# A graph layer on one core: 640 instead of 512 edges of a part taken from resident tables

## The chip, the cores and the metric

One core of one Trainium2 chip. The metric is the device time of one execution in microseconds, median of several runs.

## The reference, cut to what matters

`x` has 12500 rows (nodes) of 128 numbers; there are 412500 edges, `src` to `dst`, sorted by `dst`. For each edge a small gate is computed from the difference of its two rows, and the gated differences are summed by target:

```python
theta = x[dst] - x[src]
w = sigmoid(relu(theta @ W1 + b1) @ W2 + b2)
agg = segment_sum(w * theta, dst)
indeg = segment_sum(1, dst)
out = layernorm(x + agg + indeg * (x @ W4 + b4))
```

Since W1 is linear, a table z in DRAM holds for each node its product with W1 beside its row; an edge then needs the z row of its source, and W1's product for its target.

## The kernel before, in words

**Parts and blocks.** The edges are cut into 276 consecutive *parts*; two parts make a *block*, whose targets lie in a window of 104 nodes. The first 18 parts are *plain*: 1024 edges each, all fetched by GpSimd with eight indirect gathers (L401, 128 rows each) into one of five `zbuf`. The 258 parts behind them hold CE = 1532 edges: 512 *hot* edges that are not gathered, and up to 1024 others in 128 x 8 slots that are (two slots of a pair share a target). Parts are fetched three or four ahead.

**Hot edges.** The first 8192 rows of x stand in SBUF as 32 tables of 256 rows, each split into three bf16 terms (`tabs`). A part takes 16 hot edges from each table, 8 from each of its two half lists. For eight parts and four tables at a time (a *fetch*, about one a part), the rows' numbers are loaded and spread over all partitions (`hot_load`), compared with the partitions' numbers (`hot_tiles`, L1039, tile `of`), and multiplied with the tables (`hot_products`, L1055: 24 bf16 matmuls into a PSUM bank `pd`). `hot_out` (L1069, ScalarE) copies the columns into `xT`, the 512 hot source rows of a part, turned. Per part then: `hot_turned` multiplies them with -W1 (L1105) and adds the targets' products by a one-hot (L1106) into the bank `pz`; `hot_relu` (L1111, ScalarE) makes `hr`; `hot_rows` multiplies `hr` with w2, four matmuls that give one column each (L1119), and turns the rows back (L1122); `hot_weights` takes the sigmoid of four columns (L1128) and weighs the rows (L1131, ScalarE).

**The gathered edges.** `spread_y` multiplies one-hots of the targets with their W1 products (L893); `logits` on VectorE subtracts, applies relu and w2, and sums (L951, L956, L962) and makes one-hots of the target nodes (L926); `weigh_rest` weighs the gathered rows on ScalarE (L993, `wx`). `add_block` and `begin_block` add all weighed rows of a block into the bank `pa` by these one-hots (L1158).

**Placing.** Which edges are hot is found on VectorE, for 64 parts at a time (a *set*; before there are five sets behind the plain parts: four of 64 parts and one of two), on 128 half lists in 128 partitions. In `place` a loop over the 32 tables raises the candidates of the next table above all others by an exclusive-or of some bits (L583), takes the eight largest (MAX, L586) and strikes them out (MATCH_REPLACE, L589). The generator yields after each piece; the main loop spends a *credit* on such pieces at the end of each part (2.5 a part, with costs of 0.85 for "k", 0.5 for "x", 2.5 to 3.5 for larger ones).

**Order.** `early_part(s)` writes out the order of the plain parts, `part(s)` that of the others, engine by engine: each engine takes its instructions in exactly that order. In `part(s)` the hot work is for part t = s + 1. `issue` interleaves the sums (L1158) with the table products (L1055) on TensorE in four pieces.

## Time and profile before

| | us |
|---|---|
| median of three runs (2940.52 to 2944.18) | 2941.33 |
| the profiled execution | 2943.8 |
| its span, first to last instruction | 2942.0 |
| TensorE busy / weight loads busy | 2548.2 / 2012.3 |
| VectorE / ScalarE / GpSimd busy | 2380.3 / 2123.8 / 2164.5 |

A row of a group names line, engine, operation, tiles and shapes, then count, busy time in us, mean ns of one, and the engine's idle time just before it with what ended it. In a timeline a row has the start, the time to the end of the last of its instructions, and in brackets the idle time before. A TensorE instruction's shown length is that of its way through the array; the spacing of starts is what a stream of them costs.

### The profile page before, as it was taken

How to read it: one execution, taken by the hardware profiler on the slowest of the kernel's cores; microseconds unless marked ns; L12 is line 12 of the kernel's file. 1: busy time of each engine (PE TensorE's matmuls, PEld its weight loads, DVE VectorE, ACT ScalarE, POOL GpSimd, SP SyncE). 2: the span in 40 equal slices, each digit the busy share in tenths (PEclk: the TensorE clock that was granted, in tenths of full speed). 3: DMA queues.
4: the chain of work that ended last, by engine and by line, in shares of the span. 5: the costliest groups of instructions: out<-in, count | busy, mean ns of one | idle time of the engine just before them, and what ended most of it. 6: DMA issues, size and time to landing. Idle time of an engine off the chain costs nothing.

```text
span 2942.0 us, 59129 instructions
## 1 busy us (share of the span) xinstructions
PE 2548.2 (87%) x18606; PEld 2012.3 (68%) x18606; DVE 2380.3 (81%) x4436; ACT 2123.8 (72%) x6416; POOL 2164.5 (74%) x2213
## 2 busy tenths in 40 slices
PE   6877899988888998998898888898998888888886
PEld 5656677777676777776776666676776666677764
DVE  7899699888957988888558888888568888888654
ACT  6365778767777777677777777776777777677776
POOL 4566777777777777777777777777777777777774
PEclk8688999989999999999999999999999999999998
DMA  8455555555554555554554545454554555555542
GB/s 285 151 153 123 142 139 138 140 135 137 140 146 134 137 140 140 133 141 135 143 150 133 135 133 141 132 141 134 143 142 128 140 132 141 133 138 141 141 134 77
DMA packets 239329, 413.58 MB, mean 141 GB/s; under 512 B 63423, under 2 KB 147226, under 8 KB 237470
## 3 DMA queue, kind: packets, MB, share of 16 engines
q0 software_dynamic: 105280, 286.93, 35.3%
q1 hardware_dynamic: 131756, 116.40, 15.3%
q10 hardware_dynamic: 1970, 6.40, 0.7%
q8 instruction: 148, 2.42, 0.3%
q14 instruction: 175, 1.43, 0.2%
HBM read 388.57 MB, written 20.94 MB: 139 GB/s over the span
## 4 chain that ended last, share of the span: by engine, by line
PE 38%; ACT 19%; DVE 15%; DMA 11%; issue 7%; POOL 1%; DVEq 0%; SPq 0%; ACTq 0%; POOLq 0%
PE pa L1158 14%; DMA zbuf<-z,src_i 10%; DVE zbuf L951 5%; PE y L893 5%; PE pd L1055 5%; ACT wx L993 5%; PE px L1119 4%; ACT wxh L1131 4%; PE pz L1105 3%; PE pz L1106 3%; PE pz L1122 3%; ACT oh L872 2%; ACT oh L873 2%; ACT xT L1069 1%; ACT a L1213 1%
## 5 line engine op out<-in xcount | busy, mean ns | idle before, releaser
L401 POOL DMA_INDIRECT zbuf<-z,src_i x2060 | 2018.5, 980 | 637.0 <-issue 236.6
L993 ACT ACTIVATE wx<-zbuf,wx 128x128 f32<-128x128 f32 x2060 | 630.2, 388 | 0.0
L1158 PE MATMUL pa<-wx,ow 128*104 128x260 f32 (+1 forms) x2284 | 628.4, 393 | 0.0
L893 PEld LDWEIGHTS y<-y,oh 128*128 128x128 f32 (+1 forms) x2156 | 276.1, 197 | 420.5 <-DVE zbuf L951 378.2
L1055 PEld LDWEIGHTS <-tabs 128*128 128x128 bf16 x6360 | 452.8, 101 | 124.2 <-issue 8.2
L951 DVE TENSOR_TENSOR zbuf<-y,zbuf 128x1024 f32<-128x1024 f32 x258 | 315.1, 1221 | 272.2 <-DMA zbuf<-z,src_i 270.9
L1055 PE MATMUL pd<-of,tabs 128*128 128x128 bf16 (+3 forms) x6360 | 535.2, 223 | 0.0
L1111 ACT ACTIVATE hr<-pz 128x512 f32<-128x512 f32 x258 | 152.9, 593 | 522.9 <-PE pz L1106 522.8
L893 PE MATMUL y<-y,oh 128*128 128x128 f32 (+1 forms) x2156 | 314.7, 291 | 228.7 <-DVE zbuf L951 220.6
L1158 PEld LDWEIGHTS pa<-wx,ow 128*104 128x104 f32 x2284 | 342.8, 179 | 40.6 <-issue 0.4
L962 DVE TENSOR_REDUCE lg<-zbuf 128x8 f32<-128x1024 f32 x273 | 329.8, 1208 | 13.2
L956 DVE SCALAR_TENSOR_TENSOR zbuf<-zbuf,fix 128x1024 f32<-128x1024 f32 x273 | 331.6, 1215 | 9.3
L1158 PE MATMUL pa<-wxh,owh 128*104 128x130 f32 x2064 | 329.0, 296 | 0.0
L1131 ACT ACTIVATE wxh<-pz,wxh 128x128 f32<-128x128 f32 x1032 | 295.2, 369 | 42.1 <-PE pz L1122 35.9
L1105 PE MATMUL pz<-xT,wni 128*128 128x512 f32 x516 | 278.5, 621 | 1.6 <-ACT wxh L1131 1.6
L1158 PEld LDWEIGHTS pa<-wxh,owh 128*104 128x104 f32 x2064 | 274.3, 186 | 0.0
L1119 PEld LDWEIGHTS px<-w_c,hr 128*128 128x128 f32 x2064 | 263.5, 200 | 7.8 <-ACT hr L1111 7.8
L1119 PE MATMUL px<-w_c,hr 128*128 128x1 f32 x2064 | 262.1, 248 | 5.6 <-ACT hr L1111 5.6
L1106 PE MATMUL pz<-oh,y 128*128 128x512 f32 x516 | 264.5, 594 | 0.1
L872 ACT ACTIVATE oh<-to_all,away,mine 128x512 f32<-128x512 bf16 (+1 forms) x257 | 213.6, 831 | 3.1 <-DMA to_all<-off_d 3.1
L1106 PEld LDWEIGHTS pz<-oh,y 128*128 128x128 f32 x516 | 98.2, 191 | 124.3 <-issue 123.4
L1122 PE MATMUL pz<-wni,xT 128*128 128x128 f32 x1032 | 176.3, 297 | 0.0
(304 smaller groups left out, 3595.8 us busy)
## 6 DMA issues: line engine op xcount, KB each, us to landing
to_all<-off_d SPq DMA_DIRECT2D x258, 128.0 KB
zbuf<-z,src_i POOLq DMA_INDIRECT x2060
hot_src<-hot_s SPq DMA_DIRECT2D x228, 128.0 KB
y<-z SPq DMA_DIRECT2D x270, 28.0 KB
xw<-in_x_dram SPq DMA_DIRECT2D x138, 52.0 KB
out_dram<-o SPq DMA_DIRECT2D x138, 52.0 KB
wx<-in_x_dram ACTq DMA_DIRECT2D x12, 512.0 KB
z<-zbuf SPq DMA_DIRECT2D x6, 1024.0 KB
```

The lines of the kernel that those rows point to most:

```text
L401: ins = nc.gpsimd.indirect_dma_start(out=rows_of(s)[:, k, :], out_offset=None, in_=z if s >= NH else x, in_offset=IndirectOffsetOnAxis(ap= ...
L893: nc.tensor.matmul(y[:, j, :], d["oh"][:, (k0 + j) * P:(k0 + j + 1) * P], y_of(s), start=True, stop=True)
L951: nc.vector.tensor_sub(half, yy.to_broadcast([P, 2, n, D]), half)
L956: nc.vector.scalar_tensor_tensor(h[:, at, :], h[:, at, :], 0.0, w2.to_broadcast([P, n, D]), op0=OP.max, op1=OP.mult)
L962: nc.vector.tensor_reduce(lg[:, at, 0], h[:, at, :], AX.X, OP.add)
L993: weighed[0] = nc.scalar.activation(wx[:, k, :D], rows_of(s)[:, k, D:], AF.Copy, scale=wx[:, k, D:D + 1])
L1055: steps_of.append(lambda q=q, i=i, t=t, j=j: nc.tensor.matmul(to[:, q], tabs[:, g, i, q, t, :], of[:, t, q], start=j == 0, stop=j == HT * ...
L1105: nc.tensor.matmul(pz, wneg, xT, start=True, stop=False)
L1106: nc.tensor.matmul(pz, y_of(t), blocks[t // SUB]["oh"][:, BP:], start=False, stop=True)
L1119: nc.tensor.matmul(lgh()[:, t % SUB, q:q + 1], hr[:, at], w2_c, start=True, stop=True)
L1131: nc.scalar.activation(wx[:, q, :D], pz[:, q * P:(q + 1) * P], AF.Copy, scale=wx[:, q, D:D + 1])
L1158: return [lambda i=i, one=one, w=w: nc.tensor.matmul(to if len(w.shape) == 3 else to[:, 0, :], one, w, start=first and i == 0, stop=last a ...
```

## The change

One more of every four tables is asked twice: of each group of four tables the first gives 32 hot edges a part instead of 16. That makes 640 hot edges a part, 320 in each half list, so that parts hold CE = 1608 edges and there are 246 instead of 258 behind the plain ones, in four sets (three of 64, one of 54). With it goes:

- **PSUM.** 640 columns of f32 don't fit into a bank. The products with W1 of the two half lists go to two banks, `pz` and `halves[1]` (named px in the rows), 320 columns each, in four matmuls instead of two; the one-hots of each half list stand on 64 of the 128 partitions, with the y rows loaded to both halves of the partitions (four loads a block). The same for the y matmuls of the gathered edges.
- **Logits.** Five matmuls with w2 repeated 32 times as weights and 128 columns of `hr` moving, each into a strip of 32 partitions of `pz`, instead of four that give a column each. A sigmoid over 256 columns (`hot_gates`, ScalarE), two transposes back (`hot_gates_turned`, TensorE), and a copy of five columns precede the weighing of five, not four, times 128 rows.
- **Table products.** Still 24 matmuls a fetch, of which six now have 256 columns; the fourth table's go to the end of `halves[1]`, copied out at the end of the part (`last_out`).
- **Order.** Sums and table products are no longer interleaved: logits, turning, table products, gate transposes, sums. `hot_out` comes before `hot_relu`.
- **Placing.** Forty pairs of MAX and MATCH_REPLACE instead of 32 a set, over 805 instead of 767 columns. The exclusive-or is a TENSOR_TENSOR with a constant column in PSUM (`steps_c`), except in the first set, where it stays a TENSOR_SCALAR. Credits 2.8 a part instead of 2.5 (6.5 instead of 5.5 in the plain parts).
- **One-hots of target nodes** in plain parts from the fifth on are made by ScalarE (Abs, then Relu, ten instructions a part) instead of two TENSOR_TENSOR on VectorE.
- **Room.** Two instead of three `wx`, three instead of four `hot_src`, four instead of five `xw`, one `owh`; hot rows are loaded two parts ahead of their tiles instead of three.

TensorE in the order of the program, before: one part between the table products of the part ahead and those of its own (tiles: `xT` hot rows, `oh` one-hots, `y` target rows and result, `hr` relu's output, `w_c` w2, `wni` -W1 and the identity, `pa` the block's sums).

```order
L1055 MATMUL pd<-of,tabs 128x16x8
L1105 MATMUL pz<-xT,wni 128x512
L1106 MATMUL pz<-oh,y_150 128x512
L893 MATMUL y<-y_145,oh 128x128 x4
L1119 MATMUL px<-w_c,hr 128x1 x4
L1122 MATMUL pz<-wni,xT 128x128 x4
L1158 MATMUL pa<-a,sh 104x130
L1158 MATMUL pa<-wxh,owh 104x130 x2
L1055 LDWEIGHTS tabs
L1055 MATMUL pd<-of,tabs 128x16x8
```

The same place of the changed program, from the end of one part's table products (the weight loads are L1094 LDWEIGHTS) to the start of the next ones:

```order
L1094 MATMUL px<-of,tabs 128x128
L1177 MATMUL pz<-wni,hr 128x128
L1180 MATMUL pz<-wni,hr 128x32
L1217 MATMUL pa<-a,sh 104x130
L1217 MATMUL pa<-wxh,owh 104x130 x10
L1217 MATMUL pa<-wx_79,ow 104x260 x4
L1148 MATMUL pz<-xT,wni 128x320
L1148 MATMUL px<-xT,wni 128x320
L1151 MATMUL pz<-oh,y_142 128x320
L1151 MATMUL px<-oh,y_142 128x320
L917 MATMUL y<-y_145,oh 128x128 x4
L1165 MATMUL pz<-hr,w_c 32x128 x5
```

All sums now stand in one run behind the gate transposes (L1177, L1180), and the node products are four instructions into two banks.

ScalarE in an even part, before, from the relu to the weighing of the gathered rows (`wxh` weighed hot rows, `lg` the gathered edges' logits):

```order
L1111 ACTIVATE hr<-pz 128x512
L1069 ACTIVATE xT<-pd 128x12x32
L1069 ACTIVATE xT<-pd 128x4x32
L872 ACTIVATE oh<-to_all,away,mine 128x512
L873 ACTIVATE oh<-oh 128x512
L1128 ACTIVATE wxh<-px,b_c 128x4
L1131 ACTIVATE wxh<-pz,wxh 128x128 x4
L975 ACTIVATE wx_79<-lg,b_c 128x8
L979 ACTIVATE wx_79<-rel 128x4
L993 ACTIVATE wx_79<-zbuf_179,wx_79 128x128 x8
```

and in the changed program:

```order
L1109 ACTIVATE xT<-pd 128x10x32
L1157 ACTIVATE hr<-pz 128x320
L1157 ACTIVATE hr<-px 128x320
L892 ACTIVATE oh<-to_all,away,mine 128x640
L893 ACTIVATE oh<-oh 128x640
L1172 ACTIVATE hr<-pz,b_c 128x256
L1187 ACTIVATE wxh<-pz 128x5
L1190 ACTIVATE wxh<-pz,wxh 128x128 x2
L1190 ACTIVATE wxh<-px,wxh 128x128 x3
L1109 ACTIVATE xT<-px 128x4x8
L1109 ACTIVATE xT<-px 128x12x8
L1009 ACTIVATE wx_78<-lg,b_c 128x8
```

The copies from `pd` moved ahead of the relu; the sigmoid of the gates (L1172) and the copies from px at the end are new.

The diff, cut to its core:

```diff
-CE = 1532
+CE = 1608
+RU = RG + 1
-HK = HR * HS
+HK = HR // RG * RU * HS
...
         for r in range(HR):
             if r:
-                v.tensor_scalar(bits, bits, ((r - 1) ^ r) << FIELD, None, op0=OP.bitwise_xor)
+                if i:
+                    k = ((r - 1) ^ r).bit_length() - 1
+                    v.tensor_tensor(bits, bits, steps_c[:, k:k + 1].to_broadcast([P, WL]), op=OP.bitwise_xor)
+                else:
+                    v.tensor_scalar(bits, bits, ((r - 1) ^ r) << FIELD, None, op0=OP.bitwise_xor)
                 yield "x"
-            eight = tops[:, r, :]
-            v.max(eight, left)
-            v.tensor_scalar(eight, eight, FLOOR, None, op0=OP.max)
-            yield "k"
-            v.match_replace(left, eight, left, TAKEN)
-            yield "k"
+            for _ in range(1 if r % RG else 2):
+                eight = tops[:, u, :]
+                u += 1
+                v.max(eight, left)
+                v.tensor_scalar(eight, eight, FLOOR, None, op0=OP.max)
+                yield "k"
+                v.match_replace(left, eight, left, TAKEN)
+                yield "k"
...
-                nc.sync.dma_start(to[h * HALF:h * HALF + SW, :], rows)
+                for g in range(SUB) if b * SUB >= PLAIN else (h,):
+                    nc.sync.dma_start(to[g * HALF:g * HALF + SW, :], rows)
...
+                if s >= PLAIN:
+                    at = slice(s % SUB * HALF, (s % SUB + 1) * HALF)
+                    oh, rows = oh[at], rows[at]
...
+                if NH <= s < PLAIN:
+                    for k in range(J):
+                        nc.scalar.activation(ow[:, k, :], fix[:, :WB], AF.Abs, scale=-1.0,
+                                             bias=rel[:, k0 + k, i:i + 1])
+                    nc.scalar.activation(ow, ow, AF.Relu, scale=-1.0, bias=1.0)
...
         def hot_turned(t):
             xT = xT_all[:, (t - PLAIN) % HX, :]
-            nc.tensor.matmul(pz, wneg, xT, start=True, stop=False)
-            nc.tensor.matmul(pz, y_of(t), blocks[t // SUB]["oh"][:, BP:], start=False, stop=True)
+            oh = blocks[t // SUB]["oh"][:, BP + t % SUB * HKL:][:, :HKL]
+            banks = pz[:, :HKL], halves[1][:, :HKL]
+            for l, to in enumerate(banks):
+                nc.tensor.matmul(to, wneg, xT[:, l * HKL:(l + 1) * HKL], start=True, stop=False)
+            for l, to in enumerate(banks):
+                at = slice(l * HALF, (l + 1) * HALF)
+                nc.tensor.matmul(to, y_of(t)[at], oh[at], start=False, stop=True)
...
-                nc.tensor.matmul(lgh()[:, t % SUB, q:q + 1], hr[:, at], w2_c, start=True, stop=True)
+                nc.tensor.matmul(rowed(q), w2_c.to_broadcast([P, ST]), hr[:, at], start=True, stop=True)
...
+        def hot_gates(t):
+            nc.scalar.activation(parts[t]["hr"][:, :2 * P], pz[:, 2 * P:], AF.Sigmoid, bias=b2_c)
+
+        def hot_gates_turned(t):
+            gates = parts[t]["hr"]
+            nc.tensor.transpose(pz[:, 2 * P:3 * P], gates[:, :P], ident)
+            for q in range(G, HQ):
+                at = slice((q - G) * ST, (q - G + 1) * ST)
+                newest[0] = nc.tensor.transpose(pz[:, 2 * P + q * ST:2 * P + (q + 1) * ST],
+                                                gates[at, P:2 * P], ident[at, at])
...
-            credit[0] = min(credit[0] + 2.5, 5.0)
+            credit[0] = min(credit[0] + 2.8, 5.0)
...
+            while opened:
+                hot_out(*opened.pop(0))
             if t < NS:
                 hot_relu(t)
...
-            issue(sums, products_of_tiles())
+            if tiled:
+                products_of_tiles()
...
+            if t < NS:
+                hot_gates(t)
+                hot_gates_turned(t)
+            if h == 0 and PLAIN // SUB <= b - 1 < NK:
+                add_block(b - 1)
+            if h == 1 and b < NK:
+                begin_block(b)
...
+            last_out()
```

228 lines of the change are left out of this document (126 added, 102 removed).

## The prediction, on record before the changed kernel ran

> **What bounds the kernel now.** I read the page first, then the groups of the steady stretch from 800 to 2800 us (each shape apart).
>
> ```profile
> span 2942.0 us, 59129 instructions
> L401 POOL DMA_INDIRECT zbuf<-z,src_i x2060 | 2018.5, 980 | 637.0 <-issue 236.6
> ```
> ```profile
> L401 POOL DMA_INDIRECT zbuf<-z,src_i x1558 | 1525.7, 979 | 475.0 <-issue 180.8 <-ACT wx L993 107.9 <-DMA zbuf<-z,src_i 46.3
> L951 DVE TENSOR_TENSOR zbuf<-y,zbuf 128x1024 f32<-128x1024 f32 x195 | 238.6, 1223 | 215.4 <-DMA zbuf<-z,src_i 215.1
> ```
>
> POOL looks 74% busy, but 1525.7 + 475.0 = 2000.7 us: busy and idle of the gathers fill the whole 2000 us, one gather every 1.284 us. L951 runs once a part: 2000/195 = **10.26 us a part**, and eight gathers are 8 x 1.284 = 10.27. DVE's long idle time in front of it is ended by the gathers' DMA. So GpSimd's issue of gathers sets the pace. The timelines show that the idle time is a fixed step, and what lengthens a gather:
>
> ```profile
> 1617.46 1.96 POOL L401 DMA_INDIRECT zbuf<-z,src_i  x1 [0.30 <-issue]
> 1619.72 0.95 POOL L401 DMA_INDIRECT zbuf<-z,src_i  x1 [0.30 <-ACT sw L1232]
> ```
> ```profile
> 1618.04 0.55 DVE L583 TENSOR_SCALAR ew<-ew 128x767 int32<-128x767 int32 x1
> ```
>
> The same 0.30 us stands before each, whatever is named; a gather that meets DVE's exclusive-or (L583) takes 1.96 instead of 0.95 us.
>
> How far are the others behind? The windows, then PE's timeline in the one stretch where GpSimd was ahead and the others caught up:
>
> ```profile
> 100.00:200.00 100.00, 79.01 (x376) 60.30 (x375) 92.55 (x191) 54.71 (x133) 66.99 (x65) 0.76 0.50 138
> 400.00:500.00 100.00, 94.19 (x739) 74.54 (x738) 96.88 (x169) 82.04 (x256) 76.53 (x78) 1.00 0.53 141
> 1400.00:1500.00 100.00, 91.08 (x673) 72.63 (x671) 58.09 (x94) 75.36 (x235) 76.03 (x79) 0.95 0.50 139
> 1700.00:1800.00 100.00, 85.52 (x658) 65.94 (x657) 86.72 (x148) 72.81 (x223) 76.22 (x79) 1.00 0.51 137
> ```
> ```profile
> 402.94 1.16 PE L893 MATMUL y<-y,oh 128*128 128x128 f32 x8 [0.43 <-DVE zbuf L951]
> ...
> 494.39 1.16 PE L893 MATMUL y<-y,oh 128*128 128x128 f32 x8 [0.33 <-DVE zbuf L951]
> ```
>
> The columns are PE, PEld, DVE, ACT, POOL busy, granted clock, DMA. In 400:500 PE ran 94%, DVE 97%, at clock 1.00. The two rows are the even parts' y matmuls, the first and last of six, five blocks (ten parts) apart: 91.45/10 = **9.15 us a part**. So the others are only 1.1 us a part behind GpSimd. The change makes GpSimd's share smaller and theirs larger; that is the question.
>
> **The change, part by part.** My base is the profiled execution's 2943.8 us (span 2942.0), 2.5 us above the median of 2941.33. 258 parts x 10.26 = 2647 us; the other 297 us (start, the 18 plain parts, tail) I hold fixed save for one term below.
>
> *Fewer parts.* 412,500 edges less 18,432 are 394,068; by 1608 instead of 1532 that is 246 parts instead of 258. Gathers from z there fall from 2060 to 245 x 8 + 2 = 1962.
>
> *GpSimd.* Where no exclusive-or runs (2080 to 2180 us), a gather is cheaper:
>
> ```profile
> L401 POOL DMA_INDIRECT zbuf<-z,src_i x80 | 76.7, 958 | 24.4 <-issue 7.3 <-ACT wx L993 6.1 <-ACT oh L872 2.1
> ```
>
> (76.7 + 24.4)/80 = 1.264 us. The exclusive-or behind the first set takes the column form, with its second operand in PSUM; no trace here shows whether that form holds GpSimd up. At best all gathers cost 1.264: **10.11 us a part**. At worst 1.284: 10.27.
>
> *TensorE.* From a stretch without large waits I read the spacing of starts:
>
> ```profile
> 441.74 0.63 PE L1122 MATMUL pz<-wni,xT 128*128 128x128 f32 x4
> 442.21 0.39 PE L1158 MATMUL pa<-a,sh 104*104 104x130 f32 x2
> ...
> 443.22 0.86 PE L1158 MATMUL pa<-wxh,owh 128*104 128x130 f32 x6
> 443.92 0.50 PE L1055 MATMUL pd<-of,tabs 128*128 128x128 bf16 x6
> 444.25 0.87 PE L1158 MATMUL pa<-wxh,owh 128*104 128x130 f32 x6
> ...
> 447.42 1.08 PE L1105 MATMUL pz<-xT,wni 128*128 128x512 f32 x2
> 448.33 1.02 PE L1106 MATMUL pz<-oh,y 128*128 128x512 f32 x2
> 449.19 1.05 PE L893 MATMUL y<-y,oh 128*128 128x128 f32 x8
> 450.08 1.01 PE L1119 MATMUL px<-w_c,hr 128*128 128x1 f32 x8
> 450.95 0.63 PE L1122 MATMUL pz<-wni,xT 128*128 128x128 f32 x4
> 451.65 0.22 PE L1170 MATMUL pa<-b_t,third 65*104 65x128 bf16 x1
> ...
> 455.25 1.08 PE L1105 MATMUL pz<-xT,wni 128*128 128x512 f32 x2
> ```
>
> An f32 matmul is two instructions here. A part's hot work is 0.91 (L1105) + 0.86 (L1106) + 0.89 (y) + 0.87 (logits) + 0.47 (turning, 441.74 to 442.21) = 4.00. Sums and table products are 442.21 to 447.42 = 5.21 in an even part and 451.65 to 455.25 = 3.60 in an odd one. That is (5.21 + 3.60 + 8.00)/2 = 8.41 a part; the measured 9.15 has 0.74 of waits on top. The changes per part:
> - node products: four instructions of 320 columns for two of 512 (0.455 each): 4 x 0.284 = 1.14, **+0.23**.
> - their one-hot halves (64 rows each, two banks): one after the other 4 x 0.269 = 1.08, +0.22; side by side 0.54, -0.32; one pass overlapping its neighbour, three steps, 0.81, -0.05.
> - logits: ten instructions of 128 columns, near the 0.70/6 = 0.117 of the 130-column ones (443.22 to 443.92): 1.17, +0.30; five column strips side by side two rounds of two passes, 0.47, -0.40; each pass beside its neighbour's, six steps, 0.70, -0.17.
> - a fifth turning, 0.47/4: +0.12. Two transposes of gates: +0.24.
> - table products: six of 24 get 256 columns, at most 0.336/6 = 0.056 (443.92 to 444.25) more each: +0.34.
> - two more hot sums a block: 4 x 0.117/2 = +0.23.
>
> Sum: +0.44 with full overlap, **+0.94** with neighbours overlapping, **+1.68** with none, so 8.85, 9.35 or 10.09 a part; with the same 0.74 of waits 9.59, 10.09 or **10.83**. The y matmuls lose half their rows; I leave them at 0.89.
>
> The Trainium skill, "TensorE: Matmul & The Clock Gate" (Part 3: Packing small matmuls), says that matmuls on different row or column groups of the array run concurrently; by it the sum would be nearer +0.44 than +1.68. No run here shows two such neighbours.
>
> *A new wait.* PE now turns the gates only after ScalarE's sigmoid, with the sums and the next part's products queued behind it. Cover on PE: 0.59 of turning and 1.34 + 0.34 of table products, 2.27. On ScalarE the one-hot (L872, L873) and the sigmoid stand ahead. The nearest ScalarE rows:
>
> ```profile
> L1111 ACT ACTIVATE hr<-pz 128x512 f32<-128x512 f32 x195 | 115.7, 593 | 407.4 <-PE pz L1106 407.3
> L1069 ACT ACTIVATE xT<-pd 128x320 f32<-128x320 f32 x42 | 18.7, 444 | 0.0
> L1069 ACT ACTIVATE xT<-pd 128x256 f32<-128x256 f32 x42 | 13.9, 393 | 0.0
> L872 ACT ACTIVATE oh<-to_all,away,mine 128x512 f32<-128x512 bf16 x195 | 161.9, 830 | 3.1 <-DMA to_all<-off_d 3.1
> L873 ACT ACTIVATE oh<-oh 128x512 f32<-128x512 f32 x195 | 122.9, 630 | 6.2
> ```
>
> One-hot 0.83 + 0.63 plus a sigmoid near 0.39 is 1.85, under the 2.27: cost nothing, and if the cover went, at most 0.3 us a part, 74 us. ScalarE's additions: two relus of 320 for one of 512, 2 x 0.444 - 0.593 = 0.30; the sigmoid 0.39; two copies of the last columns and a fifth weighing, each under that 0.39, some 0.3; together about 1.6. In 400:500 it was busy 82.04 us in 100/9.15 = 10.9 parts, 7.5 a part. So 9.1: loaded, not the bound.
>
> *VectorE.* Per part it has 58.09 x 10.26/100 = 5.96 without placing, and 86.72 x 10.26/100 = 8.90 with it (1700:1800), so 2.94 of placing: credit 2.5 buys 2.5/2.2 = 1.14 rounds of exclusive-or 0.5 and two steps of 0.85. After, credit 2.8 over four rounds of cost 10.5 (five pairs, as each fourth round has two) buys 1.07 exclusive-ors and 1.33 pairs. The exclusive-or in column form is nearest to
>
> ```profile
> L577 DVE TENSOR_TENSOR ew<-ew,ed 128x767 int32<-128x767 int32 x3 | 2.9, 958 | 0.1
> ```
>
> which scaled to 805 columns is 1.0 us, against some 0.57 now. Pairs cost (2.94 - 1.14 x 0.57)/1.14 = 2.01, and 5% more for 805 columns. So placing is 1.07 x 1.0 + 1.33 x 2.11 = 3.88, with +0.13 for 208 more columns of hot one-hots a block: **9.97** in those stages. At the 97% that 400:500 reached this is 10.3 a part, at or a little above GpSimd.
>
> *The opening* is DVE's (92.55 of 100 in 100:200). Place gains eight pairs, 8 x 2.11 = 17 us, and 5% on the rest; fourteen parts' plain one-hots go to ScalarE, which has room (54.71):
>
> ```profile
> L926 DVE TENSOR_TENSOR ow<-fix,rel 128x416 f32<-128x416 f32 x34 | 18.5, 582 | 1.9 <-PE pa L1158 1.9
> ```
>
> 28 x 0.582 = 16 us off. With the larger opening tiles I take **+10 us** (from 0 to 25).
>
> *Other moves.* SP issues four y loads and four row loads a block instead of two and two, two blocks ahead of their use; the hot rows come two parts ahead of their tiles instead of three. DMA engines are half busy (0.50 to 0.53 in the windows): nothing. Two instead of three wx buffers: the sums that free one end before the next weighing; nothing.
>
> **Sum.** GpSimd asks 10.11 a part, DVE 10.3 where it places, PE 10.09 to 10.83. No row shows neighbours overlapping, the 64-row y matmuls of the plain parts are alone on the array; I take the middle of the PE pair, **10.5 us a part**: 246 x 10.5 + 297 + 10 = **2890**. Break-even is (2943.8 - 307)/246 = 10.72 us a part.
>
> **The rivals.**
> - *GpSimd stays the bound*: tiles overlap, PE needs 10.09 or less. 246 x 10.11 + 307 = 2794. For: GpSimd is so regular today. Against: DVE's 97% of 400:500.
> - *Nothing overlaps* (slower): the place is PE between the node products and the sums; price +1.68, 10.83 a part, 2664 + 307 = 2971. It decides beyond +1.57 (10.72 a part). For: the two passes of one matmul share a strip, so they must follow each other. Against: other passes may move in.
> - *The array empties whenever the tile size changes* (slower): full, 64 rows, 32 columns, full, 32 rows, full are five changes a part. The price of one is what a lone matmul lasts beyond its spacing:
>
> ```profile
> L1055 PE MATMUL pd<-of,tabs 128*128 128x128 bf16 x4684 | 404.5, 224 | 0.0
> ```
> 0.224 - 0.056 = 0.17, five times 0.84; with neighbours overlapping 10.09 + 0.84 = 10.93 a part, 2689 + 307 = 2996. It decides from four changes on. Against it, in the plain parts such a change shows no gap (48 instructions, then 64-row ones that start before the last has ended):
>
> ```profile
> 238.24 1.93 PE L1055 MATMUL pd<-of,tabs 128*128 128x112 bf16 x48
> 240.10 1.16 PE L893 MATMUL y<-y,wxh 64*128 64x128 f32 x8
> ```
> The Trainium skill, "TensorEngine Tiling (Array Packing)" (Key Properties), says that a change of tiling mode drains TensorE. By that rule this rival would come true; the two rows speak for a short drain at most.
>
> **How the numbers follow.** Forecast (10.3 to 10.7 a part, 2840 to 2935) 0.35; GpSimd bound 0.22; no overlap 0.20 and drains 0.17, both slower; 0.06 falls within 0.2% of now, about what a measurement of this kernel can tell from no change. So faster 0.57, same 0.06, slower 0.37. The range runs from 2785, just under the GpSimd case, to 3015, above both slow ones; the forecast's own is 2840 to 2935.
>
> **What would show it.** After the change: GpSimd's gathers with waits longer than 0.30 (forecast) or without (rival); their mean near 958 ns if the column form leaves them alone; spacing of the 32-column logits, 0.117 or less an instruction; gaps on PE at 64-row and 32-column neighbours; idle time before the gate transposes. Wrong would make it: a wait that I have as covered, above all ScalarE behind its weighing when the relu is due, or PE below clock 1.00.

## The result, and the profile after

The changed kernel takes **3108.16 us** (median of four runs, 3101.23 to 3123.1) against 2940.93 for the kernel before in the same comparison: a ratio of 1.0578, 95% interval 1.0536 to 1.062. It is slower by 167 us, where some 54 us less were forecast, and lies above the range, which ended at 3015. The profiled execution is the one of 3101.23 us.

The page after, its span and the group of the gathers:

```profile
span 3099.5 us, 63736 instructions
...
L408 POOL DMA_INDIRECT zbuf<-z,src_i x1962 | 1875.6, 956 | 867.6 <-ACT wx L1027 380.8
```

Gathers are fewer (1962) and shorter (956 ns, not 980), but the idle time ahead of them grew, and ScalarE's weighing (L1027), which frees the buffers, ends most of it. GpSimd is no longer the bound. The groups and the waits from 800 to 2800 us (a row of waits has total, times, longest):

```profile
L408 POOL DMA_INDIRECT zbuf<-z,src_i x1444 | 1380.3, 956 | 620.5 <-ACT wx L1027 279.9 <-issue 158.7 <-ACT xT L1109 40.0
L981 DVE TENSOR_TENSOR zbuf<-y,zbuf 128x1024 f32<-128x1024 f32 x182 | 222.0, 1220 | 2.0 <-DMA zbuf<-z,src_i 0.9 <-issue 0.7
```
```profile
POOL zbuf L408 <- ACT wx L1027: 279.9, 349, 28.3
DVE a L1282 <- ACT xuT L840: 277.8, 75, 8.3
...
ACT wxh L1187 <- PE pz L1180: 207.6, 174, 3.7
PE y L917 <- DVE zbuf L981: 162.1, 90, 9.6
...
ACT hr L1157 <- PE px L1151: 109.3, 91, 2.2
```

VectorE no longer waits for gathers ahead of L981 (215 us before, 0.9 now). Instead TensorE, VectorE and ScalarE wait for each other in a ring. 182 parts in 2000 us are 11.0 us a part, where 10.5 were forecast. The windows show in which stages:

```profile
448.80:777.50 328.70, 298.49 (x2253) 237.25 (x2251) 287.90 (x465) 252.24 (x813) 219.59 (x231) 0.91 0.49 129
1086.50:1397.70 311.20, 279.82 (x2253) 221.86 (x2252) 287.45 (x465) 252.42 (x815) 219.53 (x232) 0.97 0.51 137
1813.90:2142.90 329.00, 298.47 (x2253) 237.23 (x2251) 287.81 (x465) 252.35 (x815) 219.35 (x231) 0.91 0.49 129
2333.70:2997.30 663.60, 616.79 (x4998) 490.16 (x4997) 390.03 (x618) 552.46 (x1792) 486.15 (x511) 0.97 0.54 143
```

In the first and the third row, where placing extracts the second and the fourth set, the granted clock (last column but two) is 0.91; in the second row (third set) it is 0.97; in the last nothing is placed, and it is 0.97. The spacing of the relu in the same four stages, from ScalarE's rows of L1157 (count, then first to last start):

```profile
L1157 ACT ACTIVATE hr<-pz x30: 418/437/438, 448.8 to 777.5; 128x320 f32<-128x320 f32 x30
...
L1157 ACT ACTIVATE hr<-pz x30: 416/437/438, 1086.5 to 1397.7; 128x320 f32<-128x320 f32 x30
...
L1157 ACT ACTIVATE hr<-pz x30: 415/437/438, 1813.9 to 2142.9; 128x320 f32<-128x320 f32 x30
...
L1157 ACT ACTIVATE hr<-pz x65: 413/437/441, 2333.7 to 2997.3; 128x320 f32<-128x320 f32 x65
```

That is 11.33, **10.73**, 11.34 and, without placing, **10.37** us a part. What happens in the slow ones is seen in TensorE's timeline, an even part (first half of the rows) and the odd one behind it:

```profile
642.29 2.04 PE L917 MATMUL y<-y,oh 64*128 64x128 f32 x8 [2.16 <-DVE zbuf L981]
644.26 1.06 PE L1165 MATMUL pz<-hr,w_c 128*32 128x128 f32 x10
...
649.40 0.28 PE L1177 MATMUL pz<-wni,hr 128*128 128x128 f32 x1
...
655.89 1.05 PE L917 MATMUL y<-y,oh 64*128 64x128 f32 x8
656.87 0.62 PE L1165 MATMUL pz<-hr,w_c 128*32 128x128 f32 x10
...
659.69 0.28 PE L1177 MATMUL pz<-wni,hr 128*128 128x128 f32 x1
```

The same work, y to gate transposes, takes 649.40 - 642.29 = 7.1 us behind a pause of 2.16 us and 659.69 - 655.89 = 3.8 us without one. The windows of the two stretches name the reason, the clock:

```profile
642.29:649.40 7.11, 7.11 (x48) 6.01 (x48) 6.97 (x12) 4.92 (x10) 5.22 (x6) 0.52 0.64 170
655.89:659.69 3.80, 3.80 (x49) 3.39 (x47) 2.38 (x5) 3.44 (x9) 2.88 (x4) 1.00 0.36 105
```

So here a late VectorE costs twice: the pause, and 3.3 us of half speed behind it. A part's y matmuls are eight instructions; I count an eight as slowed when it is shown with more than 1.5 us (usual are 1.05, before 1.16). From 400 us on the trace has 188 eights with a pause under 1.5 us ahead, none slowed; with 1.5 to 4 us 20 of 46 are; with 4 us or more, six of six. The kernel before waited as long for VectorE in all, but in more and shorter waits (its row stands first; total, times, longest), and only eight of its eights were slowed behind such a pause:

```profile
PE y L893 <- DVE zbuf L951: 220.6, 174, 8.9
```
```profile
PE y L917 <- DVE zbuf L981: 222.2, 120, 9.6
```

The Trainium skill, "TensorE: Matmul & The Clock Gate" (Part 1), gives one idle window of about 3.4 us, free-running, for the fall to half; here pauses from 1.5 us on did it, and not each of them. The trace shows what mostly decides. Its clock changes only on a fixed grid of 3.41 us. From 400 us on, the clock fell after none of the 574 full-speed steps of this grid in which TensorE was busy over 70%, after 29 of the 90 in which it was busy 40 to 70%, and after all 29 below 40%. So a pause counts by how much of one such step it takes up.

### The profile page after: what moved, and what is told of

It is laid out like the page before. It is cut to its first block, busy times and chain, and to the rows that moved or that the text cites. A ratio compares the mean times of both kernels' runs of the same rounds, so it can differ in the third digit from the quotient of the medians.

```text
span 3099.5 us, 63736 instructions
## 1 busy us (share of the span) xinstructions
PE 2686.2 (87%) x20496; PEld 2135.6 (69%) x20496; DVE 2314.7 (75%) x4094; ACT 2356.7 (76%) x7465; POOL 2016.6 (65%) x2115
## 4 chain that ended last, share of the span: by engine, by line
PE 51%; ACT 15%; DVE 14%; DMA 5%; issue 3%; POOL 2%; DVEq 0%; SPq 0%; POOLq 0%; ACTq 0%
PE pa L1217 17%; PE pd L1094 8%; PE y L917 6%; DVE zbuf L981 4%; DMA zbuf<-z,src_i 4%; PE pz L1165 3%; PE pz L1151 3%; ACT wxh L1190 3%; ACT wx L1027 3%; PE pz L1168 2%; POOL zbuf L408 2%; PE px L1168 2%; PE px L1148 2%; PE pz L1148 2%; PE px L1094 2%
## 5 line engine op out<-in xcount | busy, mean ns | idle before, releaser
L1027 ACT ACTIVATE wx<-zbuf,wx 128x128 f32<-128x128 f32 x1962 | 600.1, 388 | 0.0
L917 PE MATMUL y<-y,oh 64*128 64x128 f32 x2058 | 310.5, 297 | 232.8 <-DVE zbuf L981 222.2
L917 PEld LDWEIGHTS y<-y,oh 64*128 64x128 f32 x2058 | 282.1, 204 | 318.3 <-DVE zbuf L981 283.2
L1094 PEld LDWEIGHTS <-tabs 128*128 128x128 bf16 x6072 | 459.1, 105 | 36.8
L1094 PE MATMUL pd<-of,tabs 128*128 128x256 bf16 (+3 forms) x4554 | 421.0, 253 | 0.0
L992 DVE TENSOR_REDUCE lg<-zbuf 128x8 f32<-128x1024 f32 (+1 forms) x261 | 315.0, 1207 | 13.6 <-ACT wx L1027 0.5
L986 DVE SCALAR_TENSOR_TENSOR zbuf<-zbuf,fix 128x1024 f32<-128x1024 f32 (+1 forms) x261 | 316.6, 1214 | 11.1 <-ACT ow L952 1.6
L981 DVE TENSOR_TENSOR zbuf<-y,zbuf 128x1024 f32<-128x1024 f32 x246 | 299.3, 1217 | 4.2 <-DMA zbuf<-z,src_i 2.3
L892 ACT ACTIVATE oh<-to_all,away,mine 128x640 f32<-128x640 bf16 (+1 forms) x245 | 215.7, 880 | 27.5 <-DMA to_all<-off_d 27.5
L1157 ACT ACTIVATE hr<-pz 128x320 f32<-128x320 f32 x246 | 106.0, 431 | 153.1 <-PE px L1151 153.1
L1190 ACT ACTIVATE wxh<-px,wxh 128x128 f32<-128x128 f32 x738 | 218.0, 377 | 0.0
L1151 PE MATMUL pz<-oh,y 64*128 64x320 f32 x492 | 198.0, 482 | 4.3 <-ACT oh L893 4.3
L1165 PE MATMUL pz<-hr,w_c 128*32 128x128 f32 x2460 | 173.0, 304 | 29.7 <-ACT hr L1157 29.5
L1151 PE MATMUL px<-oh,y 64*128 64x320 f32 x492 | 198.0, 482 | 0.0
```

The lines of the kernel that those rows point to most:

```text
L892: nc.scalar.activation(oh, blocks[b]["to_all"][:, c0:c1], AF.Abs, scale=mine, bias=away)
L917: nc.tensor.matmul(y[:, j, :], oh[:, (k0 + j) * P:(k0 + j + 1) * P], rows, start=True, stop=True)
L981: nc.vector.tensor_sub(half, yy.to_broadcast([P, 2, n, D]), half)
L986: nc.vector.scalar_tensor_tensor(h[:, at, :], h[:, at, :], 0.0, w2.to_broadcast([P, n, D]), op0=OP.max, op1=OP.mult)
L992: nc.vector.tensor_reduce(lg[:, at, 0], h[:, at, :], AX.X, OP.add)
L1027: nc.scalar.activation(wx[:, k, :D], rows_of(s)[:, k, D:], AF.Copy, scale=wx[:, k, D:D + 1])
```

## Experiments

None of the kernels leaves out work. Twelve of the eighteen runs fell on three chips on which the kernel before itself takes 4040 to 4133 us; there ("low-clock chips" below) TensorE's clock is granted at 0.81 to 0.84, and it stands for its own issue for hundreds of us; VectorE has time to spare, so I conclude nothing on VectorE's order from these runs. Why these chips differ is not shown. In the other six runs 0.91 to 0.93 is granted, as in the first comparison. The changed kernel itself is in none of these comparisons. Each run is compared with the kernel before on its own chip.

| run | us | before | ratio (95%) |
|---|---|---|---|
| y_late | 4177.44 | 4132.8 | 1.0162 (1.0079 to 1.0246) |
| even_place | 4242.17 | 4132.8 | 1.0311 (1.0227 to 1.0396) |
| ow_dve | 4246.58 | 4132.8 | 1.0336 (1.0248 to 1.0425) |
| xor_ts | 4244.36 | 4132.8 | 1.0315 (1.0231 to 1.0399) |
| y_late_b | 3342.53 | 2938.09 | 1.1369 (1.1348 to 1.139) |
| load_after | 3094.17 | 2938.09 | 1.0548 (1.0507 to 1.0589) |
| ow_dve_b | 3100.42 | 2938.09 | 1.0554 (1.0527 to 1.0581) |
| three | 3319.96 | 2938.09 | 1.1291 (1.1271 to 1.1312) |
| place_early | 4291.98 | 4039.91 | 1.0616 (1.0536 to 1.0695) |
| load_split | 4275.51 | 4039.91 | 1.0566 (1.0488 to 1.0644) |
| early_9 | 4303.16 | 4039.91 | 1.0636 (1.0557 to 1.0715) |
| xor_ts_b | 4301.27 | 4039.91 | 1.0626 (1.0546 to 1.0705) |
| logits_early | 3081.95 | 2938.38 | 1.0494 (1.0464 to 1.0523) |
| logits_split | 3051.42 | 2938.38 | 1.04 (1.0368 to 1.0432) |
| xor_ts_c | 4292.27 | 4043.75 | 1.0638 (1.058 to 1.0696) |
| credit_low | 4299.84 | 4043.75 | 1.0648 (1.0589 to 1.0707) |
| last_late | 4322.43 | 4043.75 | 1.0713 (1.0654 to 1.0772) |
| five | 4309.72 | 4043.75 | 1.0682 (1.0624 to 1.074) |

### y later on TensorE: y_late, y_late_b

```diff
-            spread_ahead(s)
             if t < NS:
                 hot_rows(t)
             if tiled:
                 products_of_tiles()
+            spread_ahead(s)
```

> Only TensorE's order changes: the y matmuls of the part after next stand behind the logits, the turnings and the table products instead of ahead of them, so the rows that VectorE must have subtracted by then (which free the y banks) are needed some 3.5 us later in each part. Theory L (a loop: VectorE late in the even part, TensorE idle before y, its granted clock then halves for some 7 us, ScalarE's relu late, VectorE idle in the odd part): the idle time before y goes, the clock in the placing stages comes back to 0.97 or more, a part there falls from 11.3 to 10.3 to 10.5 us, and over 192 parts the time falls by 150 to 190 us, to 2920 to 2960. Theory W (VectorE's longer placing work is itself the bound in those stages): the time stays within 20 us of the changed kernel's 3108, with VectorE near 97% busy in the placing stages.

> The y_late kernel once more, because TensorE stood for its own issue on the chip of the first four runs, where the kernel before itself took 4133 us. With the kernel before near 2941 us: theory L (VectorE late, TensorE idle before y, half clock, late relu, VectorE idle) gives 2920 to 2960, with the idle time before y under 100 us in all and the clock of the placing stages at 0.97; theory W (VectorE's longer placing work is the bound) gives 3090 to 3125.

On the first chip it was the fastest of four (65 to 69 us under the other three). On the second it took 3342.53 us, where load_after and ow_dve_b, without this edit, took 3094 and 3100. The waits of y_late_b:

```profile
PE pz L1165 <- ACT hr L1157: 358.1, 245, 9.1
```

No wait of the y matmuls for L981 is left, as theory L had it; but TensorE now waits for ScalarE's relu in 245 of 246 parts, 1.46 us each. The y matmuls had hidden the relu. A part takes some 12 us with placing and without. Both expectations fell, and theory L as I had put it (take the wait away and the time comes down) with them: the cover of another wait was lost.

### VectorE's order: logits_early, place_early, even_place

logits_early leaves TensorE's order alone and moves VectorE's rows of the next part ahead of the placing steps:

```diff
-            if s < NS:
+            if s == PLAIN:
                 logits(s)
...
                 weigh_rest(s)
+            if s + 1 < NS:
+                logits(s + 1)
             fetch_step(s)
             spend("kxspmz")
```

> VectorE's relu rows of part s+1 (subtraction, weighted relu, reduction, target one-hots) are issued in part s ahead of the placing steps and of the block's normalization, instead of in part s+1 behind them. TensorE's and ScalarE's order stay. Theory L2 (order): TensorE's idle time ahead of y, 370 us in the changed kernel, falls under 100; VectorE still waits in the odd part but no one waits for it; a placing part takes 10.3 to 10.6 us instead of 11.3, and the time falls by 130 to 190 us to 2920 to 2975. Theory W (sum): VectorE is as late with the placing as before, a placing part stays at 11.0 to 11.4 us, the time within 30 us of 3095 to 3108.

Windows and relu rows of logits_early, for the second and the fourth set:

```profile
459.80:763.80 304.00, 271.87 (x2184) 217.17 (x2184) 277.59 (x444) 241.99 (x784) 210.71 (x222) 0.97 0.51 136
1825.50:2132.50 307.00, 275.78 (x2184) 220.37 (x2184) 277.65 (x444) 242.07 (x784) 210.47 (x222) 0.94 0.51 135
```
```profile
L1157 ACT ACTIVATE hr<-pz x29: 416/437/437, 459.8 to 763.8; 128x320 f32<-128x320 f32 x29
...
L1157 ACT ACTIVATE hr<-pz x29: 414/437/438, 1825.5 to 2132.5; 128x320 f32<-128x320 f32 x29
```

No wait of the y matmuls for L981 is left, the clock is 0.97, 0.97 and 0.94 in the three sets, and a part takes 10.86 and 10.96 us in the two slow sets, some 0.4 less than above; in the third it is 10.86, 0.13 more. The time fell to 3081.95, by 26 us across two comparisons (ratios 1.0494 and 1.0578), not by 130 to 190 us. The waits for VectorE came back as other waits:

```profile
PE pz L1165 <- ACT hr L1157: 190.2, 116, 8.2
ACT oh L892 <- DMA to_all<-off_d: 128.9, 42, 28.5
```

In the second set's stage TensorE was busy 271.87/28 = 9.71 us a part, against 298.49/29 = 10.29 in the changed kernel: 0.58 us of slow clock gone, and idle for 1.15 against 1.04.

Which set is slow isn't fixed, though. load_after and ow_dve_b, whose edits leave the order of TensorE, VectorE and ScalarE in these stages as it is, took 11.01, 11.31 and 10.82, and 10.82, 11.15 and 11.26 us a part in the second, third and fourth set, the changed kernel 11.33, 10.73 and 11.34. In all nine TensorE idles 1.01 to 1.08 us a part; what differs is its busy time, 9.65 us in the fastest (clock 0.97) and 10.29 in the slowest (0.91). Their mean is 11.09, so logits_early's mean of 10.89 is 0.2 us better, and no better than the fastest of the nine. So theory L2 holds for the clock and for some 26 us of the time, which lies in the range that theory W gave; it isn't the whole.

The two other edits of VectorE's order ran on low-clock chips only:

```diff
# place_early
                 logits(s)
+            if h:
+                spend("kx")
             if done_b:
                 finish(b - 1)
# even_place
-            credit[0] = min(credit[0] + 2.8, 5.0)
+            credit[0] = min(credit[0] + 5.6 * (1 - h), 5.6)
```

> y_late fell: y ahead of the logits covers the relu. Here TensorE's order stays and VectorE's changes: in odd parts the placing steps that were bought (extractions and exclusive-ors) stand behind the relu rows and ahead of the block's total, which waits some 5 us for ScalarE's copy of the turned rows, instead of behind it. Theory L2 (VectorE's work would fit, but it stands idle in its order ahead of the total and then places when the next even part's subtraction is due): the placing fills the idle time, TensorE's 370 us of idle ahead of y falls under 150, a placing part takes 10.4 to 10.7 us instead of 11.3, and the time falls by 110 to 170 us to 2935 to 3000. Theory W (VectorE's work itself is the bound) or a total that comes later and holds ScalarE's rows up by as much: within 25 us of 3108.

> The same placing work per block, but all of it bought in the even part (credit 5.6 there and none in the odd part, where VectorE has the hot target one-hots, the block's total and its normalization). Theory L: VectorE is no longer late for the subtraction of the even part, which comes before the placing steps, so TensorE's idle time ahead of y falls, and a placing part takes 10.4 to 10.8 us instead of 11.3; 3108 falls by 90 to 170 us to 2940 to 3020. Theory W: the sum of VectorE's work is the same, so the time stays within 20 us of 3108.

place_early took 4291.98 us, even_place 4242.17. Each is within 0.3% of a kernel of the same comparison that moves none of the placing (xor_ts_b, xor_ts). Neither can tell the theories apart on a chip where VectorE isn't short of time.

### VectorE's sum: xor_ts (three times), credit_low

```diff
# xor_ts, xor_ts_b, xor_ts_c
-                if i:
+                if False:
# credit_low
-            credit[0] = min(credit[0] + 2.8, 5.0)
+            credit[0] = min(credit[0] + (2.8 if s < PLAIN + S2 - 8 else 2.4), 5.0)
```

> The exclusive-or takes the form with a number in every set, as the kernel before has it, instead of the PSUM column behind the first. It is some 0.4 us shorter on VectorE, but holds up a gather that meets it by about 1 us. Theory L or W, with GpSimd no longer the bound (its gathers wait for buffers): VectorE has 0.4 x 1.07 = 0.43 us a part less in the placing stages, and the time falls by 30 to 80 us to 3030 to 3080, though the gathers' mean rises from 956 to about 980 ns. The rival (the gathers' buffers are tight, so a longer gather delays the part): the time rises by 0 to 50 us to 3108 to 3160.

> The xor_ts kernel once more on another chip. VectorE has some 0.4 us less for each exclusive-or in the placing stages, GpSimd's gathers that meet one take about 1 us more. Theory W or L2: the time falls by 30 to 80 us to 3020 to 3080. The rival (the gathers' buffers are tight): it rises to 3110 to 3160.

> The changed kernel with the number form of the exclusive-or in every set. Theory W: VectorE has 0.4 x 1.04 = 0.4 us a part less in the extractions, so at the same 92% busy a part there takes 0.45 us less than the 11.3, 10.7 and 11.35 of the three sets; over 87 parts 39 us less in all: 3060 to 3080. If the gathers that meet the exclusive-or (1.96 instead of 0.95 us) hold the parts up, or VectorE isn't the bound, 3095 to 3125.

> From the second placed set on, a part may buy 2.4 of placing instead of 2.8, so the same work is spread over some 55 parts instead of 47. Theory W: VectorE has 6.1 + 3.9 x 2.4/2.8 = 9.45 us a part in the extractions instead of 10.0, which at 92% busy is 10.3 us, as in the parts without placing; the two sets gain 20 to 35 us each: 3035 to 3070. If not VectorE's work but the order decides, a part with placing stays at 11 us and there are more of them: 3100 to 3125.

All four fell on low-clock chips (4244.36, 4301.27, 4292.27, 4299.84 us), so the question that they were made for, whether VectorE's sum is the bound of the placing stages, stays open. A window and waits of xor_ts_c show how it is there:

```profile
1300.00:1400.00 100.00, 75.44 (x475) 58.62 (x474) 51.28 (x100) 55.28 (x179) 48.09 (x49) 0.81 0.36 93
```
```profile
ACT hr L1172 <- remote: 839.2, 171, 7.8
...
PE px L1094 <- issue: 471.1, 610, 1.9
```

VectorE is half idle in a placing stage, ScalarE's sigmoid waits, and TensorE stands 471 us ahead of table products for no cause that the profile shows. One thing can be read: a gather took 965 to 967 ns with the number form in all sets against 959 to 961 with the column form (place_early, credit_low, last_late), so the column form spares GpSimd, a little.

### The one long wait: load_after, load_split

Near 1712 us ScalarE's one-hot (L892) waits 27.5 us once for its row `to_all`, while SyncE issues the edges of the last set.

```diff
# load_after: the edges behind the block's loads
-            if s in turns:
-                edges[s + 3] = turns[s], load(turns[s])
...
                 fetch(b + 2)
+            if s in turns:
+                edges[s + 3] = turns[s], load(turns[s])
# load_split: 54 rows as 48 and 6
-                nc.sync.dma_start(t[h * S2:h * S2 + full, :m], bass.AP(
-                    tensor=edges.tensor, offset=edges.offset + e0 + h * HL, ap=[[CE, full], [1, m]]))
+                for r0, r1 in ((0, full // 16 * 16), (full // 16 * 16, full)):
+                    if r0 < r1:
+                        nc.sync.dma_start(t[h * S2 + r0:h * S2 + r1, :m], bass.AP(
+                            tensor=edges.tensor, offset=edges.offset + e0 + r0 * CE + h * HL,
+                            ap=[[CE, r1 - r0], [1, m]]))
```

> In the part that loads a set's edges, SyncE first issues the loads of the block after next and then the edges, instead of the other way round; nothing else changes. If the 27 us by which ScalarE's one-hot waits for its row once, near 1712 us, come from the edge load standing ahead in SyncE's queue, that wait goes and the time falls by 20 to 30 us to 3080 to 3090. If the row is late for another reason, or if the edges, landing later, then hold the placing up by as much, the time stays within 10 us of 3108.

> load_after did not remove the one long wait: the row, issued ahead of the edges, landed 50 us late while the DMA engines were mostly idle. Here the loads of the last set's 54 rows are cut into 48 rows and 6 (a multiple of 16 and the rest); sets of 64 rows are as before. If 54 rows are spread over few of the 16 DMA engines, whose queues then hold every other transfer up, the wait of 25 us near 1712 us goes and the time falls by 20 to 30 us to 3065 to 3090. If the cause is another (the single rows, the four-byte loads), it stays within 10 us of 3095 to 3108.

SyncE's issues in load_after:

```profile
1713.06 0.60 SPq L827 DMA_DIRECT2D to_all<-off_d  x1
...
1714.60 5.45 SPq L191 DMA_DIRECT2D es<-in_src_dram  x1
1720.15 9.40 SPq L188 DMA_DIRECT2D ed<-in_dst_dram  x2
1729.59 9.35 SPq L191 DMA_DIRECT2D ed<-in_dst_dram  x1
```

The row is issued first now, and still ScalarE waits for it 22.18 us, until 1763.34: 50 us after its issue. While it waits, the DMA engines are half idle or more (share and GB/s are the last columns):

```profile
1745.00:1750.00 5.00, 0.00 (x0) 0.00 (x0) 0.00 (x0) 0.00 (x0) 1.89 (x2) 0.61 0.50 137
1750.00:1755.00 5.00, 0.00 (x0) 0.00 (x0) 0.14 (x1) 0.00 (x0) 0.00 (x0) 0.50 0.09 27
```

So it is not SyncE's order, and not the DMA's total; pieces of the row that stand behind the edges on single engines would fit. With 48 and 6 rows the wait is gone: in load_split and in logits_split and five, which carry the same edit, and in no other run (16.9 to 28.5 us in the others). load_split's time is 16 to 28 us under the three others of its comparison. In logits_split the longest wait for a row is 5.9 us (with logits_early's edit alone it was 28.5):

```profile
ACT oh L895 <- DMA to_all<-off_d: 108.2, 44, 5.9
```

That the 54-row loads block the row is shown; how, isn't. A share of 0.09 is 1.4 of 16 engines. The Trainium skill, "DMA: Bandwidth & Descriptors" (Why a DMA increments its semaphore by 16 and not by 1), states that a DMA uses the largest number of engines up to 16 that divides its rows: 9 for 54, 16 for 48, 6 for 6. The direction agrees with the runs; nine engines alone don't make 50 us of it, and no view here shows the single engines.

### The opening: ow_dve, early_9, last_late

The first relu of a hot part comes at 349 us, at 293 before, 56 us later instead of 10.

```diff
# ow_dve, ow_dve_b
-                if NH <= s < PLAIN:
+                if False:
# early_9
-            credit[0] = min(credit[0] + 6.5, 6.5) if s < PLAIN - 5 else 200.0
+            credit[0] = min(credit[0] + 9.0, 9.0) if s < PLAIN - 5 else 200.0
# last_late (with ow_dve's edit)
-            if s < PLAIN - 1:
-                last_out()
             advance("p")
             gate_sums(s)
             weigh(s)
+            if s < PLAIN - 1:
+                last_out()
```

> The plain parts' target one-hots go back to VectorE (one comparison each); all else is the changed kernel's. Theory O1 (the 56 us that the opening lost come from ScalarE's one-hots standing in its order, each waiting for VectorE and holding its weighing and copies behind it): the first relu of a hot part, at 349 us in the changed kernel, comes at 300 to 320, and the time falls by 30 to 50 us to 3058 to 3078. Theory O2 (the opening is longer because placing the first set has eight more pairs and larger tiles): VectorE gets 16 us more work, the first relu comes at 345 to 365, and the time is 3105 to 3125.

> The ow_dve kernel once more, for the same reason. Theory O1 (ScalarE's one-hots in the plain parts hold the opening up): first relu of a hot part at 300 to 320 us instead of 349, time 3058 to 3078. Theory O2 (eight more pairs and larger tiles in the first set): first relu at 345 to 365, time 3105 to 3125. On the first chip the first relu moved by 4 us only, from 384 to 380, which speaks for O2.

> The opening's parts may buy 9.0 of placing each instead of 6.5; nothing else changes. Theory O3 (placing the first set is not done when the opening's last parts come, so its rest, the sorting network above all, is run in one go near 299 to 313 us with TensorE idle for 14 us and ScalarE for 10): the first relu of a hot part comes at 320 to 335 us instead of 349, the time falls by 12 to 30 us. Theory O2 (VectorE's sum of work in the opening decides, wherever it stands): no change beyond 8 us.

> The opening alone: in its parts ScalarE copies the last columns of the table products behind the weighing instead of ahead of it (where it waits for TensorE's products, 54 us in all between 200 and 349 us), and the target one-hots are VectorE's again. If that wait holds the weighing and so the next sums up, the first relu comes at 300 to 325 us instead of 341 (with the one-hots alone), and the time is 3060 to 3085. If the copy is late without holding anything, the first relu stays at 338 to 345 us and the time at 3090 to 3105.

With ow_dve_b the first relu comes at 341 us, between the two theories: 8 us of the 56, near O2's side; its time is no better than that of load_after in the same comparison (3100.42 and 3094.17). With ow_dve it is 379.9 us, against 383.8 of xor_ts on its chip. early_9 moved nothing (389.1 us against 388.6 of xor_ts_b on its chip): O3 fell. last_late made it later, 410.8 against 385.6 of xor_ts_c on the same chip: the copy that I took for the obstacle is waited for sooner than the weighing. The windows say that work is the smaller part of it. The changed kernel's:

```profile
100.00:200.00 100.00, 76.83 (x325) 59.54 (x325) 95.53 (x169) 56.35 (x145) 52.76 (x55) 0.67 0.42 115
200.00:300.00 100.00, 65.98 (x432) 50.45 (x431) 65.89 (x156) 67.14 (x182) 45.61 (x48) 0.75 0.38 106
```

Before, VectorE was busy to the end (94% from 200 us on); here it is to 200 us, and from there only 66%, with TensorE at a clock of 0.75. Up to the first relu VectorE is busy 267.5 us (254.4 before): its work grew by 13 us, near the 10 forecast; the other 43 us are idle time. Three rows of a plain part of the changed kernel, one from each engine's timeline:

```profile
254.59 2.07 PE L917 MATMUL pz<-y,wxh 64*128 64x128 f32 x8 [6.87 <-ACT wxh L881]
```
```profile
265.27 0.34 ACT L1109 ACTIVATE xT<-px 128x112 f32<-128x112 f32 x2 [6.23 <-PE px L1094]
```
```profile
265.64 0.47 DVE L696 TENSOR_SCALAR px<-ed 128x293 int32<-128x293 int32 x1 [5.80 <-ACT xT L1109]
```

TensorE waits for ScalarE, then ScalarE for TensorE's last table products, then VectorE for ScalarE's copy of them, one after the other. The copy of the last columns ties the three together; that it is the cause isn't shown, since the kernels that moved it got slower.

### Together: three, logits_split, five

three is y_late, load_after and ow_dve; logits_split is logits_early, load_split, early_9 and ow_dve; five is xor_ts, credit_low, last_late, ow_dve and load_split.

> The three edits of y_late, load_after and ow_dve together. If each acts as theories L, O1 and the queue say, their gains add: 3108 less 170, 27 and 40 is 2871, with 2850 to 2900 as the range, below the kernel before. If only L holds it is 2920 to 2960; if none, 3090 to 3125.

> logits_early, and three edits more, each with a stage of its own: the last set's loads cut into 48 and 6 rows (the wait for to_all, 22 to 27 us, should go: it went on a chip with a slow TensorE), 9.0 instead of 6.5 of placing a part in the opening, and the opening's target one-hots on VectorE. The first relu comes at 325 to 341 us if buying the first set earlier helps (341 was measured with the one-hots alone), at 341 to 350 if not. With theory L2 the whole takes 2870 to 2945 us, with theory W 3040 to 3090.

> The edits of xor_ts_c, credit_low, last_late (with the one-hots on VectorE) and the load cut into 48 and 6 rows, together. With theory W and the wait in the opening: 3100 less 25 (load), 30 (opening), 40 and 50 (placing) is 2955, with 2930 to 2985 as the range: about the kernel before, since the parts without placing take 10.2 to 10.3 us in any case, and 246 x 10.25 is 2522. If only the load and the one-hots act: 3055 to 3075.

three (3319.96) carries y_late's loss. logits_split, 3051.42, is the best version of the change: 30.5 us under logits_early in the same comparison, about the long wait of 27 to 29 us and the first relu, at 345 instead of 350 us. It still is 4.0% slower than the kernel before. five fell on a low-clock chip and shows only that its wait for `to_all` is gone. No version beat the kernel before.

## Why the prediction was wrong

Forecast and profile differ by 3101.2 - 2890 = 211 us. From the relu's first and last starts (348.75 and 3072.33 us, 245 steps; before 292.61 and 2912.55, 257 steps) the terms are: a part 11.01 us with 27 us set aside, 0.51 over the forecast, 246 times: 125. The one wait: 27. The opening, +56 instead of +10: 46. The fixed rest: the kernel before ran 10.19 us a part over its whole length, not the 10.26 of its middle, so its rest was 314 and not 297: 17. The tail is 2 shorter. Together 213, within 2 of it. Of the 125, some 55 came in the three stretches shown above and 75 in those between and ahead of them, where the other pieces of placing run and a part takes 11.1 to 12.5 us; the parts without placing, at 10.37, gave 8 back.

- **GpSimd:** right. It is no longer the bound, its gathers wait for buffers, and the column form leaves them at 956 ns (958 forecast at best). Rival 1 (GpSimd stays the bound) fell.
- **TensorE's own work:** the sum was right, two of its terms were not. An odd part without waits:

```profile
1605.19 0.70 PE L1148 MATMUL pz<-xT,wni 128*128 128x320 f32 x2
1605.73 0.70 PE L1148 MATMUL px<-xT,wni 128*128 128x320 f32 x2
1606.36 0.53 PE L1151 MATMUL pz<-oh,y 64*128 64x320 f32 x1
1606.37 0.53 PE L1151 MATMUL px<-oh,y 64*128 64x320 f32 x1
...
1607.01 1.05 PE L917 MATMUL y<-y,oh 64*128 64x128 f32 x8
1607.99 0.62 PE L1165 MATMUL pz<-hr,w_c 128*32 128x128 f32 x10
1608.55 0.44 PE L1168 MATMUL pz<-wni,xT 128*128 128x128 f32 x2
...
1611.19 0.26 PE L1228 MATMUL pa<-b_t,third 65*104 65x128 bf16 x1
...
1613.39 0.70 PE L1148 MATMUL pz<-xT,wni 128*128 128x320 f32 x2
```

From L1148 to the gate transposes' end it is 6.00 us, the sums are 2.20 here (4.29 in the even part): (4.29 + 2.20)/2 + 6.00 = **9.25** a part, close to the 9.35 that I took. That is luck: two terms were off and cancel. Tiles overlap fully, not by neighbours: the 64-row halves start 0.01 us apart, and by the starts of the single instructions four of the five 32-column strips start within 0.03 us, the fifth behind them, so that ten logits take 0.56 us. That is the +0.44, 8.85 a part. The other 0.40 is about what the changes of tile size cost. Two 320-column matmuls take 0.54 us from start to start, the next two, ahead of the 64-row ones, 0.63. Over 241 parts the median spacing grows from 0.269 to 0.363 us there, from 0.112 to 0.202 at the change to 32 columns, and from 0.109 to 0.203 at the change back: 0.09 each, where rival 3 (drains) had 0.17. So rival 2 (nothing overlaps) fell, and rival 3 is real at half its price, too small to decide. The Trainium skill's drain on a change of tiling mode, "TensorEngine Tiling (Array Packing)" (Key Properties), agrees with these 0.09 us. The two rows of the plain parts that I read as no gap hide the same: there the last start ahead of the change is 0.10 us earlier, between narrow table products 0.025.
- **"With the same 0.74 of waits": this step failed.** It was taken from a stretch at clock 1.00 and held constant. In the second set's stretch a part is 11.33 us, of which TensorE is busy 10.29: 9.25 of work, **1.04 of slow clock**, and 1.04 of waits. In the third set it is 10.73, with 0.40 of slow clock and 1.08 of waits; without placing 10.37, with 0.39 and 0.73. So where VectorE places, the waits were 0.3 more than forecast, and the clock that they cost, up to 1.04, wasn't in the sum. I had named TensorE below clock 1.00 as what would make it wrong, and gave it neither a price nor a chance.
- **The new wait** for the sigmoid, taken as covered, was: 37 us in all, 26.8 of them in one wait.
- **VectorE:** the sum was right, the way to read it wrong. 287.90/29 is 9.93 us a part, 9.91 in the third set; forecast 9.97. "At the 97% that 400:500 reached" held in no set: it was busy 88, 92 and 87%. VectorE waits for ScalarE (rows of the kernel before and of the changed one), which I had as "loaded, not the bound": 552.46/64 = 8.6 us a part, forecast 9.1. An engine can be short of the bound and still be late for the others.

```profile
DVE a L1224 <- ACT xuT L820: 51.6, 21, 6.3
```
```profile
DVE a L1282 <- ACT xuT L840: 390.6, 102, 8.3
```

- **The opening:** the +10 was a sum of VectorE's work (13 measured); 43 us of idle time weren't in it. In ow_dve_b, without ScalarE's one-hots, the first relu came 8 us earlier.
- **"Nothing"** for SyncE and the loads, since the DMA engines are half busy: wrong by 27 us, for the loads of one set in the whole kernel.
- **Open:** why a part with placing stays at 10.9 us when TensorE no longer waits for VectorE; and why the same waits cost 0.40 us of slow clock in one set and 1.04 in another, beyond the grid of the clock. VectorE at 91% (its sum) and ScalarE's rows behind late loads both stand in the traces, and the runs meant to part them fell on low-clock chips.

## What to carry to other kernels

When a change brings three engines to within 10% of each other, add up not only each one's work: give each wait that the trace shows the price of the slow clock behind it, and a chance of growing. Before moving an instruction out of a wait, ask what it covers: the y matmuls waited for VectorE and hid ScalarE's relu, and the second was worth more. And compare several stretches before calling one slow: the same order gave 10.7 to 11.3 us a part.

## What the runs showed of the hardware

- Fp32 matmuls on two row halves of the array overlap fully (0.01 us apart), and four 32-column strips start within 0.03 us; a change of tile size costs 0.09 us.
- TensorE's clock changes on a grid of 3.41 us, to half behind a step in which it was busy under 40%, sometimes behind one of 40 to 70%; most half-speed stretches last 3.4 or 6.8 us. Pauses from 1.5 us on can do it.
- The sign of an edit can depend on the chip: y_late is 1.6% faster than xor_ts at clocks of 0.82 to 0.84 (4177.44 against 4244.36), and 8% slower than load_after at 0.91 to 0.92 (3342.53 against 3094.17).
- Four loads of 54 rows kept a row issued ahead of them for 50 us, at a DMA share of 0.09 to 0.58 in the last 20 of them; as 48 and 6 rows they kept none.
